# Unscaled wavelet columns, thresholds scaled on the chip, and evictions on ScalarE in a chain of four convolutions

## The chip, the cores and the metric

The kernel runs on one core of one Trainium2 chip. The metric is the device time of one execution in microseconds (us); lower is better. The core has these engines: TensorE (PE, with its weight loads shown as PEld), VectorE (DVE), ScalarE (ACT), GpSimd (POOL) and SyncE (SP), which here issues every DMA of the program from one queue. Each engine works through its own instructions in order and waits for others by semaphores.

## The reference

The input x has 4 images of 64 channels of 256 x 256, in float32. Four layers follow one another. Layers 0, 2 and 3 are long convolutions along rows and columns, each with a filter that a small network computes from positions; layer 1 works on Haar wavelet coefficients:

```
# layers 0, 2, 3: hx, hy are one row filter and one column filter per channel
k = einsum('ijk,imk->ijmk', hx, hy)[0]            # separable 256x256 filter
out = irfft2(rfft2(x, 512) * rfft2(k, 512) / 512)[..., :256, :256] + x * bias

# layer 1
f1 = haar2d(x)
for i in range(2):
    f3 = f1 * v[i]                                 # v, tau: one number per coefficient
    f4 = einsum('bchw,oc->bohw', f3, conv_w[i])    # mixes the 64 channels
    acc += sign(f4) * relu(abs(f4) - tau[i])       # soft threshold
out = haar2d(acc, inverse=True) + x
```

## The kernel before

Each convolution is a product with Toeplitz matrices, along rows and then along columns, on PE. Work goes in rounds of two channels of two images: a tile is [128, 8, 256], one "big" tile of 1 MB. Two groups of two images make 64 rounds.

**Phase A** (`phase_a`, loop over 64 rounds, each of ten "pieces") does layer 0 and the forward wavelet transform. A round's pieces 0 to 3 are row products (`rows`, PSUM tiles a1ps, copied to ay by ACT, L460), 4 and 5 the wavelet transform across rows of an earlier round (`product`, one small product with forward_sb into a3ps), 6 to 9 the column products (`columns`, a2ps). The transform along a row (`forward_free`) runs on POOL. The residual x * bias is added as DVE evicts a2ps (L480). The result of `product` is evicted by DVE with a multiplication by wrow, the orthonormal scale of each wavelet column (L493), and stored to the DRAM tensor coef. SP also loads x, two rounds ahead, and the Toeplitz matrices (toep, from filt in DRAM), and stores coef.

**Phase B** (`phase_b(grp)`, once for each group, 64 steps of two units) does the mixing. A unit's three pieces are: multiply by v and subtract thresholds of the unit before (`multiply` L642, `less` L662, both DVE), and add the unit before that to its sum on POOL; then the PE products of the next unit (`mix`, L623), the sign on ACT (L648) and the final max-times-sign on DVE (`threshold`, L667); then the magnitude on ACT (L657). The tile named a, of the magnitudes, and f4, of the PE products, are in PSUM, one buffer each in the first group. `load_v` fetches v and tau of a step in one DMA from one input, in which they alternate and each is repeated for the 64 channels.

**Phase C** (`phase_c`) does the inverse transform and layers 2 and 3, in rounds of 18 pieces. `inverse_free` undoes the row transform (POOL, and DVE for the first two rounds); there each level's differences are multiplied by sqrt(half), on ACT beforehand (`scales`, L378) or within a DVE operation (L403). Half of the second group's mixing results go to DRAM without threshold (`raw`), and phase C applies the threshold itself (`shrink`) with v and tau laid out by rows (`scale_rows`).

`beside(main, side, lead, tail)` writes the order out by hand: it issues the main pieces one after the other and puts the side pieces evenly between them, from main piece `lead` to `tail` pieces before the end. The order is: the network for layer 0; phase A's first 348 pieces beside `rest` (the networks of layers 2 and 3, and the stores of filters, filt<-padded); the following 272 pieces of phase A beside phase B of group 0; a transition; phase C beside phase B of group 1; phase C alone. In each piece `flush()` first issues the evictions that the piece before put off with `later`. Since nothing is reordered, an engine's queue holds the instructions in this order.

Of the kernel before, what the change touches and what calls it, by code (L numbers as in the profile page):

```python
# [41 lines left out]
F32 = mybir.dt.float32  # L42
AF = mybir.ActivationFunctionType
ALU = mybir.AluOpType
# [3 lines left out]
P = 128  # L48
B, C, N = 4, 64, 256

ROW = 64
# [48 lines left out]
def conv_haar_kernel(  # L100
    ctx: ExitStack, tc: tile.TileContext, x, zT, w1, wbd, cols, wo, decay, wo_first, decay_first, bias, forward, inverse, wrow, pack, v, v_rows, out
):
# [13 lines left out]
    unshrunk = coefficients("unshrunk")  # L116
    filt = [dram.tile([ROUNDS, 2, REPEATS, ITEMS, PERIOD], F32, tag=f"filt{l}", name=f"filt{l}") for l in range(NL)]

# [168 lines left out]
    nc.sync.dma_start(inverse_sb, inverse)  # L287
    wrow_sb = const.tile([P, N], F32, tag="wrow", name="wrow_sb")
    nc.sync.dma_start(wrow_sb, wrow.partition_broadcast(P))
    bias_sb = const.tile([P, NL * C], F32, tag="bias", name="bias_sb")  # L290
    nc.sync.dma_start(bias_sb, bias.partition_broadcast(P))

    for p in network([0]):
        p()

    rest = []
# [3 lines left out]
    for copy in spread(1, 0, ROUNDS, REPEATS // 2) + spread(2, 0, ROUNDS, REPEATS // 2):  # L300
        rest += [lambda: None] * (2 * APART - 4) + [copy]

    TILES = [(r, c) for r in range(2) for c in range(2)]

    def half(r):
        return slice(r * ROW, (r + 1) * ROW)

# [65 lines left out]

    def scales(src):

        half = 2
        while half < N:
            nc.scalar.mul(diffs(src, half), diffs(src, half), math.sqrt(half))  # L378
            yield
            half *= 2  # L380

    def inverse_free(src, dst, name, engine, level):


        blocks = src.rearrange("p n (k q) -> p n k q", k=BLOCKS)

        cur, half = blocks[:, :, 0:1, 0], 1
        while half < N:
            o = dst
            if half < HALF:  # L390
                o = level(2 * half)
            d = diffs(src, half)
            if half < BLOCKS:
                s, pair = cur, o.rearrange("p n (t q) -> p n t q", q=2)
            else:
                s = cur.rearrange("p n (k t) -> p (n k) t", k=BLOCKS)
                pair = o.rearrange("p n (k t q) -> p (n k) t q", k=BLOCKS, q=2)
            for q, op in ((0, ALU.add), (1, ALU.subtract)):
                to = pair[:, :, :, q]
                if engine is nc.gpsimd:  # L400
                    engine.tensor_tensor(to, s, d, op)  # L401
                else:
                    engine.scalar_tensor_tensor(to, d, math.sqrt(half) * (1 - 2 * q), s, ALU.mult, ALU.add)  # L403
                yield
            cur = o
            half *= 2
# [3 lines left out]
    def later(op):  # L410

        waiting.append(op)
# [23 lines left out]
    def phase_a():  # L436
# [45 lines left out]
        def product(t, bp):  # L482
            s = st[t]
            if bp == 0:

                s["f"] = big("out", f"f_{t}", 2)
            two = banks(f"a3ps{bp}_{t}")
            fw = blocks(s["fw"])
            haar(two, lambda r, c: fw[half(r), c, 2 * bp : 2 * bp + 2], forward_sb)
            for b, ps in enumerate(two):  # L490
                f = s["f"][:, 4 * bp + 2 * b : 4 * bp + 2 * b + 2]
                w = wrow_sb.unsqueeze(1).to_broadcast([P, 2, N])
                later(lambda f=f, ps=ps, w=w: nc.vector.tensor_tensor(f, ps, w, ALU.mult))  # L493

# [45 lines left out]
    def phase_b(grp):  # L540
# [25 lines left out]
        def load_v(s):  # L566
            if s >= STEPS:
                return
            d = st[s]
            d["v"], d["tau"] = [], []  # L570

            def fetch(first, count, tag):
                n = 2 * count * W
                t = bp.tile([P, count, 2, W], F32, tag=tag, name=f"{tag}_{grp}_{first}_{s}", bufs=3)
                at = v.offset + s * P * (4 * W + PAD) + first * 2 * W
                rows = bass.AP(v.tensor, at, [[4 * W + PAD, P], [1, n]])
                nc.sync.dma_start(t.rearrange("p i k w -> p (i k w)"), rows)
                d["v"] += [t[:, i, 0] for i in range(count)]
                d["tau"] += [t[:, i, 1] for i in range(count)]
# [121 lines left out]
        def piece(u, j):  # L701

            s, i = divmod(u, 2)
            if j == 0:
                if u < units:
                    multiply(u)
                if 0 < u <= units:
                    less(u - 1)
# [8 lines left out]
                if i and raw(2 * s - 1):  # L717
                    store(s - 1)
            elif j == 1:
                if u + 1 < units:  # L720
                    mix(u + 1)
# [34 lines left out]
    def phase_c():  # L756
# [389 lines left out]
```

## Time and profile before

| | us |
|---|---|
| median of 3 runs | 2545.4 |
| lowest and highest | 2540.11, 2548.39 |
| the profiled execution, its own time | 2543.18 |
| its span in the profile | 2541.3 |

| engine | busy us | share of the span | instructions |
|---|---|---|---|
| PE | 2311.6 | 91% | 53298 |
| PEld | 1875.9 | 74% | 53298 |
| DVE | 1840.0 | 72% | 2070 |
| ACT | 1325.9 | 52% | 2190 |
| POOL | 2063.0 | 81% | 2428 |

The span runs from the first to the last profiled instruction. The DMA engines moved 679.08 MB, 267 GB/s on average over the span. TensorE's granted clock was 0.979 of full speed on average. The shares are means over stages that have different limits, so the stretches of the span have to be looked at one by one. A row of the groups reads: line, engine, operation, output <- inputs, shapes, number; after the bar the busy time in us, the mean of one in ns, and the idle time of the engine just before them with what ended it. Busy times of neighbouring instructions overlap a little, so the distance between their starts is shorter than their durations.

### The profile page before, as it was taken

Reading aid. Unit: us, or ns where it says so; the run is one execution under the profiler, and the core shown is the slowest. Engines: PE = TensorE matmul, PEld = TensorE weight load, DVE = VectorE, ACT = ScalarE, POOL = GpSimd, SP = SyncE. Lnnn points to the kernel's source line nnn. Section 1 sums busy time; section 2 is a strip of 40 time slices with the busy share of each in tenths; the row PEclk is TensorE's granted clock in tenths of the full one; section 3 lists DMA queues with packets and bytes.
Section 4 is the critical chain, followed back from the end, with each engine's and each line's share of the span. In section 5 each row is a group of like instructions: output and inputs, shape, how many; then the busy total and the mean of one; then the engine's idle time right before and its main releaser. Section 6 shows DMA issues by size and latency. Waiting matters only on the chain.

```text
span 2541.3 us, 118857 instructions
## 1 busy us (share of the span) xinstructions
PE 2311.6 (91%) x53298; PEld 1875.9 (74%) x53298; DVE 1840.0 (72%) x2070; ACT 1325.9 (52%) x2190; POOL 2063.0 (81%) x2428
## 2 busy tenths in 40 slices
PE   7999998788888888877999999999989999999999
PEld 5799996444454444555777777787889999998888
DVE  4655557799999999856777677776667777777763
ACT  1122223566666666244666666666655555556552
POOL 2889997989899999768777767676779999999990
PEclk9999999899999999888999999999999999999999
DMA  6678877799999999556888889889866666666653
GB/s 201 224 269 271 272 275 296 266 327 338 337 320 341 336 318 340 206 184 248 318 320 313 306 302 321 311 312 315 287 215 217 216 215 217 215 212 207 220 167 111
DMA packets 201798, 679.08 MB, mean 267 GB/s; under 512 B 29119, under 2 KB 30464, under 8 KB 188873
## 3 DMA queue, kind: packets, MB, share of 16 engines
q1 hardware_dynamic: 201288, 671.48, 76.3%
q8 instruction: 419, 6.86, 1.1%
q14 instruction: 91, 0.74, 0.1%
HBM read 427.63 MB, written 243.73 MB: 264 GB/s over the span
## 4 chain that ended last, share of the span: by engine, by line
PE 44%; DVE 4%; issue 2%; ACT 2%; DMA 2%; POOL 2%; SPq 1%; DVEq 0%; ACTq 0%; POOLq 0%
PE c2c L312 10%; PE c2r L312 10%; PE c1r L312 9%; PE c1c L312 8%; PE c0ps L324 4%; PE f L623 3%; DVE cy L896 1%; DVE m L667 1%; DMA g<-mixed 1%; DVE x L642 1%; DVE x L662 1%; ACT ch L877 1%; POOL i L401 1%; ACT x L657 0%; SPq L161 0%
## 5 line engine op out<-in xcount | busy, mean ns | idle before, releaser
L401 POOL TENSOR_TENSOR i<-i,g 128x16 f32<-128x16 f32 x744 | 429.9, 598 | 28.2 <-ACT g L378 1.1
L312 PEld LDWEIGHTS a2ps<-toep,ay 64*64 64x64 f32 x8192 | 315.3, 136 | 126.3 <-DVE f L493 70.0
L623 PE MATMUL f<-ft,mix 64*64 64x512 f32 x2048 | 301.7, 623 | 116.8 <-DVE x L642 99.2
L312 PE MATMUL a2ps<-toep,ay 64*64 64x128 f32 (+3 forms) x8192 | 352.8, 303 | 27.4 <-DVE f L493 27.4
L312 PEld LDWEIGHTS a1ps<-toep,x 64*64 64x64 f32 x8192 | 300.1, 134 | 66.3 <-issue 31.8
L312 PE MATMUL a1ps<-toep,x 64*64 64x64 f32 (+3 forms) x8192 | 338.1, 299 | 4.3 <-DMA toep<-filt 2.3
L312 PEld LDWEIGHTS c2c<-toep,ch 64*64 64x64 f32 x8192 | 296.8, 135 | 61.0 <-issue 28.4
L312 PEld LDWEIGHTS c1c<-toep,ch 64*64 64x64 f32 x8192 | 295.4, 133 | 52.0 <-issue 23.7
L685 POOL TENSOR_TENSOR gt<-m,ft 128x512 f32<-128x512 f32 x128 | 163.3, 1276 | 197.8 <-DVE m L667 193.5
L312 PE MATMUL c1r<-toep,z 64*64 64x64 f32 (+3 forms) x8192 | 315.0, 300 | 7.8 <-issue 3.8
L312 PEld LDWEIGHTS c1r<-toep,z 64*64 64x64 f32 x8192 | 291.2, 135 | 41.5 <-issue 19.0
L312 PE MATMUL c2c<-toep,ch 64*64 64x128 f32 (+3 forms) x8192 | 310.0, 299 | 8.6 <-ACT ch L877 6.9
L312 PE MATMUL c2r<-toep,cy 64*64 64x128 f32 (+3 forms) x8192 | 310.1, 298 | 7.9 <-issue 6.6
L312 PEld LDWEIGHTS c2r<-toep,cy 64*64 64x64 f32 x8192 | 288.9, 134 | 37.6 <-issue 20.4
L401 POOL TENSOR_TENSOR ci<-i,g 128x1024 f32<-128x1024 f32 x124 | 312.1, 2539 | 4.5
L648 ACT ACTIVATE m<-x 128x1024 f32<-128x1024 f32 x194 | 206.0, 1062 | 210.0 <-DVE x L642 103.1
L312 PE MATMUL c1c<-toep,ch 64*64 64x128 f32 (+3 forms) x8192 | 307.3, 297 | 4.1 <-ACT ch L877 2.5
L460 ACT COPY ay<-a1ps 128x512 f32<-128x512 f32 x256 | 137.3, 589 | 325.2 <-PE a1ps L312 324.6
L877 ACT COPY ch<-c2r 128x512 f32<-128x512 f32 x256 | 137.2, 589 | 285.2 <-PE c2r L312 284.4
L493 DVE TENSOR_TENSOR f<-a3ps,wrow_sb 128x512 f32<-128x512 f32 x256 | 161.3, 682 | 122.5 <-PE a3ps L324 118.6
L642 DVE TENSOR_TENSOR x<-f,v 128x1024 f32<-128x1024 f32 x192 | 233.4, 1216 | 18.1 <-PE f L623 15.3
L896 DVE SCALAR_TENSOR_TENSOR o<-cy,bias_sb,c2c 128x512 f32<-128x512 f32 x256 | 176.9, 742 | 91.8 <-PE c2c L312 87.1
(84 smaller groups left out, 3950.7 us busy)
## 6 DMA issues: line engine op xcount, KB each, us to landing
toep<-filt SPq DMA_DIRECT2D x768, 112.0 KB
ft<-coef SPq DMA_DIRECT2D x128, 512.0 KB
v<-in_v SPq DMA_DIRECT2D x64, 1024.0 KB
mixed<-gt SPq DMA_DIRECT2D x128, 512.0 KB
g<-mixed SPq DMA_DIRECT2D x256, 256.0 KB
x<-in_x SPq DMA_DIRECT2D x128, 256.0 KB
coef<-f SPq DMA_DIRECT2D x128, 256.0 KB
x<-in_x SPq DMA_DIRECT2D x32, 1024.0 KB
```

The source lines that it names most:

```text
L312: nc.tensor.matmul(ps[r][half(c), j % 2, k * ROW :], data[half(r), c, k, bass.ts(j, ROW)], t(r, c)[:, : N - k * ROW], start=k == 0, stop=k ...
L324: nc.tensor.matmul(ps[r][half(c)].rearrange("p h k -> p (h k)"), matrix[half(r)], pairs(r, c).rearrange("p h k -> p (h k)"), start=True, s ...
L401: engine.tensor_tensor(to, s, d, op)
L460: later(lambda y=y, ps=ps: nc.scalar.copy(y, ps))
L493: later(lambda f=f, ps=ps, w=w: nc.vector.tensor_tensor(f, ps, w, ALU.mult))
L623: nc.tensor.matmul(un[u]["f4"][half(q), b, :], mixers[0][half(r), bass.ts(i, C)], st[s]["f"][half(r), b], start=True, stop=True, tile_posi ...
L642: nc.vector.tensor_tensor(un[u]["x"], un[u]["f4"], both(u, "v"), ALU.mult)
L648: nc.scalar.activation(un[u]["m"], un[u]["x"], AF.Sign)
L662: nc.vector.tensor_tensor(un[u]["a"], un[u]["a"], both(u, "tau"), ALU.subtract)
L685: nc.gpsimd.tensor_tensor(g[:, 0], m[:, 0], st[s]["f"][:, 0], ALU.add)
L877: later(lambda y=y, ps=ps: nc.scalar.copy(y, ps))
L896: nc.vector.scalar_tensor_tensor(to, of, bias_sb[:, at : at + 1], ps, ALU.mult, ALU.add)
```

## The change

The wavelet columns are no longer brought to orthonormal scale. The forward matrix for the rows is divided by sqrt(256) instead, L493 becomes a plain copy on ACT, and wrow is not loaded. A coefficient now has another factor in each column, so the threshold of that column needs the same factor: tau is loaded in a small form ([128, 1024]), multiplied on DVE by per_level once (`scale_thresholds`), and stored with 64 DMAs, each to four channels (`put_thresholds`), into a new DRAM tensor thresholds. These 65 pieces are merged evenly into `rest`. `load_v` fetches v from the input and tau from thresholds, in two DMAs into the two halves of one tile. In the inverse transform the differences are multiplied by half instead of sqrt(half). In the first group only, `less` moves from the first piece of a unit to the head of the second.

```diff
-    wrow_sb = const.tile([P, N], F32, tag="wrow", name="wrow_sb")
-    nc.sync.dma_start(wrow_sb, wrow.partition_broadcast(P))
...
+    def merged(one, other):
+        both = [((k + 0.5) / len(of), p) for of in (one, other) for k, p in enumerate(of)]
+        return [p for _, p in sorted(both, key=lambda x: x[0])]
...
+    tau_sb = mp.tile([P, 2, W], F32, tag="tau", name="tau_sb")
+
+    def scale_thresholds():
+        per_level_sb = mp.tile([P, N], F32, tag="per_level", name="per_level_sb")
+        nc.sync.dma_start(per_level_sb, per_level.partition_broadcast(P))
+        nc.sync.dma_start(tau_sb.rearrange("p r w -> p (r w)"), tau)
+        rows = tau_sb.rearrange("p r (h k) -> p (r h) k", k=N)
+        nc.vector.tensor_tensor(rows, rows, per_level_sb.unsqueeze(1).to_broadcast([P, 4, N]), ALU.mult)
+
+    def put_thresholds(copies, r, i):
+        of = tau_sb[half(i), r].unsqueeze(1).to_broadcast([ROW, copies.stop - copies.start, W])
+        nc.sync.dma_start(thresholds[:, r, copies, i * W : (i + 1) * W], of)
+
+    puts = [(slice(n, n + 4), r, i) for n in range(0, C, 4) for r in range(2) for i in range(2)]
+    rest = merged(rest, [scale_thresholds] + [lambda at=at: put_thresholds(*at) for at in puts])
...
-            nc.scalar.mul(diffs(src, half), diffs(src, half), math.sqrt(half))
+            nc.scalar.mul(diffs(src, half), diffs(src, half), half**power)
...
-                    engine.scalar_tensor_tensor(to, d, math.sqrt(half) * (1 - 2 * q), s, ALU.mult, ALU.add)
+                    engine.scalar_tensor_tensor(to, d, float(half * (1 - 2 * q)), s, ALU.mult, ALU.add)
...
-                w = wrow_sb.unsqueeze(1).to_broadcast([P, 2, N])
-                later(lambda f=f, ps=ps, w=w: nc.vector.tensor_tensor(f, ps, w, ALU.mult))
+                later(lambda f=f, ps=ps: nc.scalar.copy(f, ps))
...
             def fetch(first, count, tag):
-                n = 2 * count * W
-                t = bp.tile([P, count, 2, W], F32, tag=tag, name=f"{tag}_{grp}_{first}_{s}", bufs=3)
-                at = v.offset + s * P * (4 * W + PAD) + first * 2 * W
-                rows = bass.AP(v.tensor, at, [[4 * W + PAD, P], [1, n]])
-                nc.sync.dma_start(t.rearrange("p i k w -> p (i k w)"), rows)
+                t = bp.tile([P, 2, count, W], F32, tag=tag, name=f"{tag}_{grp}_{first}_{s}", bufs=3)
+                at = slice(first * W, (first + count) * W)
+                nc.sync.dma_start(t[:, 0].rearrange("p i w -> p (i w)"), v[s, :, at])
+                nc.sync.dma_start(t[:, 1].rearrange("p i w -> p (i w)"), thresholds[s].rearrange("r c w -> (r c) w")[:, at])
...
             if j == 0:
                 if u < units:
                     multiply(u)
-                if 0 < u <= units:
+                if 0 < u <= units and grp == GROUPS - 1:
                     less(u - 1)
...
             elif j == 1:
+                if 0 < u <= units and grp < GROUPS - 1:
+                    less(u - 1)
                 if u + 1 < units:
                     mix(u + 1)
...
-                for op in scales(late["rows"][:, k].rearrange("p s (h k) -> p (s h) k", h=2)):
+                for op in scales(late["rows"][:, k].rearrange("p s (h k) -> p (s h) k", h=2), (1.0, 0.5)[k]):
...
-    signs = signs * w[order][:ROW, None]
+    signs = signs * w[order][:ROW, None] / math.sqrt(N)
...
-        "v": padded(np.repeat(v[:, :, None], C, axis=2).reshape(STEPS * P, 4 * W)),
+        "v": padded(np.repeat(by_row("v")[:, :, None], C, axis=2).reshape(STEPS, P, 2 * W)),
+        "tau": f(by_row("tau").transpose(2, 0, 1, 3).reshape(P, 2 * W)),
+        "per_level": f((1.0 / (w[order] * math.sqrt(N))).astype(np.float32)),
```

More of the change, by code (lines that the diff above doesn't have):

```diff
@@ L100, in conv_haar_kernel @@
 def conv_haar_kernel(
-    ctx: ExitStack, tc: tile.TileContext, x, zT, w1, wbd, cols, wo, decay, wo_first, decay_first, bias, forward, inverse, wrow, pack, v, v_rows, out
+    ctx: ExitStack, tc: tile.TileContext, x, zT, w1, wbd, cols, wo, decay, wo_first, decay_first, bias, forward, inverse, pack, v, tau, per_level, v_rows, out
 ):
@@ L116, in conv_haar_kernel @@
     unshrunk = coefficients("unshrunk")
+    thresholds = dram.tile([STEPS, 2, C, 2 * W + PAD], F32, tag="thresholds", name="thresholds")
     filt = [dram.tile([ROUNDS, 2, REPEATS, ITEMS, PERIOD], F32, tag=f"filt{l}", name=f"filt{l}") for l in range(NL)]
@@ L294, in conv_haar_kernel, with half @@
         p()
+    def half(r):
+        return slice(r * ROW, (r + 1) * ROW)
+    def merged(one, other):
+        both = [((k + 0.5) / len(of), p) for of in (one, other) for k, p in enumerate(of)]
+        return [p for _, p in sorted(both, key=lambda x: x[0])]
     rest = []
@@ L301, in conv_haar_kernel @@
         rest += [lambda: None] * (2 * APART - 4) + [copy]
+    tau_sb = mp.tile([P, 2, W], F32, tag="tau", name="tau_sb")
[10 more added lines that the diff above has]
+    rest = merged(rest, [scale_thresholds] + [lambda at=at: put_thresholds(*at) for at in puts])
     TILES = [(r, c) for r in range(2) for c in range(2)]
-    def half(r):
-        return slice(r * ROW, (r + 1) * ROW)
     def toeplitz(ps, data, t, j):
@@ L372, in diffs, with scales @@
         return src.rearrange("p n (k q) -> p (n k) q", k=BLOCKS)[:, :, m : 2 * m]
-    def scales(src):
+    def scales(src, power=1.0):
         half = 2
         while half < N:
-            nc.scalar.mul(diffs(src, half), diffs(src, half), math.sqrt(half))
+            nc.scalar.mul(diffs(src, half), diffs(src, half), half**power)
             yield
@@ L572, in fetch @@
             def fetch(first, count, tag):
-                n = 2 * count * W
-                t = bp.tile([P, count, 2, W], F32, tag=tag, name=f"{tag}_{grp}_{first}_{s}", bufs=3)
-                at = v.offset + s * P * (4 * W + PAD) + first * 2 * W
-                rows = bass.AP(v.tensor, at, [[4 * W + PAD, P], [1, n]])
-                nc.sync.dma_start(t.rearrange("p i k w -> p (i k w)"), rows)
-                d["v"] += [t[:, i, 0] for i in range(count)]
-                d["tau"] += [t[:, i, 1] for i in range(count)]
+                t = bp.tile([P, 2, count, W], F32, tag=tag, name=f"{tag}_{grp}_{first}_{s}", bufs=3)
+                at = slice(first * W, (first + count) * W)
+                nc.sync.dma_start(t[:, 0].rearrange("p i w -> p (i w)"), v[s, :, at])
+                nc.sync.dma_start(t[:, 1].rearrange("p i w -> p (i w)"), thresholds[s].rearrange("r c w -> (r c) w")[:, at])
+                d["v"] += [t[:, 0, i] for i in range(count)]
+                d["tau"] += [t[:, 1, i] for i in range(count)]
             fetch(0, 2 if grp < GROUPS - 1 else 1, "v")
@@ L1090 @@
     scaled = signs * w[order][:ROW, None] / math.sqrt(N)
-    signs = signs * w[order][:ROW, None]
+    signs = signs * w[order][:ROW, None] / math.sqrt(N)
     pack = a["L1_conv_conv_w"].transpose(2, 0, 1).reshape(C, P)
-    v = np.stack([by_row("v"), by_row("tau")], axis=3)
     filters = [[[r * CI, r * CI + 1, C + r * CI + h] for h in range(2)] for r in range(ROUNDS)]
@@ L1129 @@
         "inverse": f(np.concatenate([scaled] * 2).astype(np.float32)),
-        "wrow": f(w[order].astype(np.float32)),
         "pack": f(np.concatenate([pack, pack])),
-        "v": padded(np.repeat(v[:, :, None], C, axis=2).reshape(STEPS * P, 4 * W)),
+        "v": padded(np.repeat(by_row("v")[:, :, None], C, axis=2).reshape(STEPS, P, 2 * W)),
+        "tau": f(by_row("tau").transpose(2, 0, 1, 3).reshape(P, 2 * W)),
+        "per_level": f((1.0 / (w[order] * math.sqrt(N))).astype(np.float32)),
         "v_rows": f(np.stack([by_block("v"), by_block("tau")], axis=1)),
```

## The prediction

> **What bounds the kernel now.** I read the busy time by stretch first, because the shares of the whole span mix four stages. I set the borders by the kernel's loops: the first convolution alone (to about 405 us), the same beside the first mixing (to 1020), a transition, the later convolutions beside the second mixing (1200 to 1830), and these alone. Columns: stretch, its length, busy us (instructions) of PE, PEld, DVE, ACT, POOL, granted clock, mean busy share of the DMA engines, GB/s.
>
> ```profile
> 62.00:153.00 91.00, 91.00 (x2244) 73.79 (x2240) 55.78 (x85) 18.24 (x34) 79.76 (x131) 1.00 0.67 235
> 153.00:362.00 209.00, 209.00 (x5444) 198.64 (x5438) 105.95 (x160) 42.95 (x80) 188.88 (x321) 1.00 0.81 273
> ...
> 500.00:1020.00 520.00, 423.75 (x6892) 251.85 (x6884) 497.01 (x508) 337.40 (x419) 472.03 (x518) 0.99 0.95 330
> ...
> 1200.00:1830.00 630.00, 589.61 (x13902) 491.00 (x13905) 455.13 (x431) 404.42 (x702) 450.83 (x511) 1.00 0.89 312
> ```
>
> In the first stage PE is never idle and DVE is half idle; the DMA engines have a fifth to a third left. In 500 to 1020, DVE is 96% busy, but the DMA engines are 95% busy too and POOL 91%. In 1200 to 1830 PE leads again, and the last stage has PE busy throughout.
>
> Next the costliest groups, for the prices, and the waits of 500 to 1000, for who is late (us in total, times, longest).
>
> ```profile
> L493 DVE TENSOR_TENSOR f<-a3ps,wrow_sb 128x512 f32<-128x512 f32 x256 | 161.3, 682 | 122.5 <-PE a3ps L324 118.6
> L460 ACT COPY ay<-a1ps 128x512 f32<-128x512 f32 x256 | 137.3, 589 | 325.2 <-PE a1ps L312 324.6
> ```
> ```profile
> PEld a2ps L312 <- DVE f L493: 51.3, 73, 2.0
> ...
> ACT a L657 <- DVE m L667: 90.7, 75, 2.5
> ACT m L648 <- POOL gt L682: 53.3, 31, 2.2
> ```
>
> DVE is waited for by PE and ACT; no engine's list in that window names a DMA (only SP's own queue does). So DVE sets the pace, with two other resources within 5%.
>
> Then the DMA engines' own rate for the kinds of transfer that resemble the new one. All stretches below have the engines over 90% busy. The first four hold a store filt<-padded (480 KB, from partitions 0 to 63, each read several times); the fifth holds coef<-f stores (also 64 partitions, but every second of 128); the last is in the mixing stage.
>
> ```profile
> 167.00:169.50 2.50, 2.50 (x81) 2.50 (x75) 0.42 (x1) 1.07 (x2) 2.05 (x3) 1.00 0.93 255
> 188.00:190.50 2.50, 2.50 (x81) 2.50 (x76) 0.41 (x1) 1.07 (x2) 2.01 (x2) 1.00 0.93 235
> ...
> 227.00:229.50 2.50, 2.50 (x83) 2.50 (x78) 1.78 (x4) 0.00 (x0) 2.15 (x9) 1.00 0.95 280
> ...
> 268.00:270.50 2.50, 2.50 (x86) 2.50 (x81) 1.41 (x2) 0.00 (x0) 2.26 (x8) 1.00 0.99 239
> 258.00:260.00 2.00, 2.00 (x68) 2.00 (x63) 1.41 (x2) 0.00 (x0) 1.76 (x6) 1.00 0.98 372
> ...
> 727.00:731.00 4.00, 3.95 (x88) 2.74 (x83) 4.00 (x6) 2.09 (x2) 4.00 (x3) 1.00 1.02 414
> ```
>
> Equally busy engines move 252 GB/s (mean of the first four) with the padded stores, and 372 to 414 without.
>
> **The change, part by part.**
>
> *64 threshold stores in the first stage.* Each takes 512 KB (524,288 bytes) from 64 neighbouring partitions of tau_sb, each row read four times, to DRAM in runs of 2 KB. The side list is spread over the pieces 2 to 318 of the first loop, ten a round: 65 items over 31.6 rounds, 2.03 stores a round. Every round's loads of x and toep and stores of coef stand behind them in SP's queue and in the DMA engines. The nearest row is the padded store: 524,288 / 252 GB/s = 2.08 us of all engines, 4.2 us a round. The coef stores' issues give the rounds: 20 from 153 to 361, 10.4 us each, of which 0.81 x 10.4 = 8.4 us are DMA; 8 from 62 to 153, 11.4 us each, of which 7.6 us. So a late round needs 8.4 + 4.2 = 12.6 us against 10.4, +2.2 us for 21 rounds = +46; an early one 11.8 against 11.4, +0.4 for 11 rounds = +4. Sum **+50**. Low end: all of a late round's bytes (273 x 10.4 + 2.03 x 524 KB = 3.9 MB) at 414 GB/s take 9.4 us, hidden under PE: 0. High end: the engines are no fuller than the 0.95 of the mixing stage: 12.6/0.95 = 13.3 and 11.8/0.95 = 12.4, 21 x 2.9 + 11 x 1.0 = +72. I take the padded row because source, queue, direction and repeated reading are the same; coef<-f differs in its partitions.
>
> The Trainium skill, "SBUF — State Buffer", section "Door 1: The DMA port swizzle", speaks against this part: partitions 0 to 63 (or 64 to 127) reach only 8 of 16 ports, measured there as 196 GB/s at 1 MiB, and two such transfers on different halves hardly overlap. By that a store would take 2.7 us, the stage would grow by some 90 us and the whole be 2612 instead of 2572, an estimate from the page; no row here shows such a transfer alone. It would also say why coef<-f, on every second partition, runs at 372.
>
> *Evictions from DVE to ACT.* 256 of 682 ns become copies, priced by L460 at 589 ns. In the first and last stages PE sets the pace: nothing. Beside the mixing a round takes 23.5 us, from the coef stores' issues:
>
> ```profile
> L497 SPq DMA_DIRECT2D coef<-f x44: 592/598/1442, 516.2 to 1009.5; - x44
> ```
>
> (two a round, 21 intervals). DVE: a pair occupies 1.20 us (it starts at 701.12, the next operation at 702.32), so 2.4 us leave 0.956 x 23.5 = 22.5: 20.1. ACT: 0.649 x 23.5 + 4 x 0.59 = 17.6. POOL stays at 0.908 x 23.5 = 21.3. The DMA engines stay at 0.95 x 23.5 = 22.3, for the same bytes are loaded. So the next thing late is the DMA: at 0.985 busy a round takes 22.65, -0.85 us for 26 rounds (1020 - 409 over 23.5) = **-22**. Ends: with POOL as the wall 21.3, -57 (the DMA rows' own time would have to shrink); on the other side, ACT works in order and an f copy now queues behind a sign that waits for POOL (up to 2.2 us) or a magnitude that waits for DVE (up to 2.5). PE's a2ps and the mixing matmuls behind it wait for that copy, and DVE for those. If both pairs of each round expose 2.5 us: 20.1 + 5.0 = 25.1, +42.
>
> *L662 moved to the head of the next piece, first mixing only.* It now stands behind the evictions, next to L667. It gets more time for its magnitude, but is no longer parted from L667, which reads its result: 1.34 us between their starts (714.16 to 715.50) instead of 1.15, about 0.2 us for three units in five, 5 units a round: +0.6 of DVE time. 20.7 is still under 22.3, so it costs nothing; without the DMA's cover it would cost 26 x 0.6 = 16. The v tile is freed, and SP's next load issued, one eviction pair (1.3 us) later; two steps of buffers (20 us) hide that.
>
> *Loads of v and thresholds, two instead of one.* One issue more (0.54 us on SP) a step, behind which ft, coef, toep and mixed stand; SP mostly waits for compute there. In the second mixing the rows halve to 2 KB. Bounds 0 to 57 steps x 0.54 = 31; PE leads, so nearest to nothing: **+2**.
>
> *Transition.* Between 1053 and 1078 five pairs of L493 stand between the L403 steps that end in ci: 6 us of DVE less at most, 0 at least where L403 waits for DMA or PE anyway: **-3**.
>
> *The start.* The wrow load goes, two small loads and one DVE product of 128x1024 (1.2 us as L642) come, while DVE idles half of the time: 0, ends -2 and +3. Factors in scales, inverse_free and scale_rows change value, not count: 0.
>
> Sum: 50 - 22 + 2 - 3 = +27. The profiled execution took 2543.2 us (span 2541.3 and 1.9 around it), 2.2 under the median of 2545.4: 2543.2 + 27 = 2570 beside its own time, **2572** beside the median.
>
> **The rivals.**
>
> 1. *The DMA engines swallow the stores* (not slower). Place: rounds 0 to 31. Price: the store's time p. For: 19% idle late, 33% early, and coef<-f at 372. Against: the 252 GB/s rows. The first stage grows by 21 x (2.03p - 2.0) us; it equals the 23 us won elsewhere at p = 1.53 us (343 GB/s), from where the change isn't slower. At p of 1.0 or less all is hidden: 2545 - 23 = 2522.
> 2. *A store at coef's price*: 524,288/372 = 1.41 us, 8.4 + 2.9 = 11.3, +0.9 x 21 = +19, less 23: 2541, no change.
> 3. *ACT takes DVE's place in the mixing*: PE's wait for f moves from DVE to ACT and grows; half of the +42 above and no gain: 2545 + 50 + 21 - 1 = 2615. For: four f copies stand in a row on ACT. Against: ACT is only 65% busy.
> 4. *The relief doesn't show* (the DMA wall at 0.95): 2545 + 50 + 2 - 3 = 2594.
>
> **How the numbers follow.** Main case (1.5 to 2.2 us a store, some relief) 0.52, its own range 2553 to 2590; rival 1 0.19; rival 2 0.13; rival 3 0.06; rival 4 0.10. About 0.3% (7.6 us) can be told from no change. Faster (below 2538): rival 1 and the lower edge of rival 2, 0.20. Same: most of rival 2, 0.13. Slower: the rest, 0.67. The range leaves out about 0.1 below and 0.1 above: 2528 to 2610.
>
> **What would show it.** In 153 to 400 the DMA share at 0.95 or more and PE no longer full, waiting for x or toep; the first L595 later than its 406 us by about 50 (the step is wrong if by under 20). Between that and the first L403 (643 us now) some 25 us less, DVE near 0.89 busy, DMA at 0.97 or more; a DMA share below 0.95 there with a shorter round would refute the wall. PE waiting for ACT f by more than the 51 us would speak for rival 3. The prediction fails altogether if the stores run above 343 GB/s.

## The result, and the profile after

The changed kernel takes 2637.74 us (median of 4 runs, 2635.87 to 2638.49); the kernel before took 2543.12 us beside it (median of 4, 2540.11 to 2548.39). The ratio is 1.037, 95% interval 1.035 to 1.039: slower by 3.7%. The profiled execution's span is 2635.8 us against 2541.3.

Four instants cut the span into stages: the start of the fifth round of phase A (its first ay copy); the first operation on tile spare_f, where the first mixing joins (L595 before, L616 after); the first operation of the inverse transform on i_x (L403 before, L426 after); and the end.

| us | fifth round | first stage ends | mixing, to the first i_x | i_x to the end | span |
|---|---|---|---|---|---|
| before | 68.2 | 406.3 | 643.1 | 1491.9 | 2541.3 |
| after | 81.0 | 517.8 | 645.8 | 1472.2 | 2635.8 |
| difference | +12.8 | +111.5 | +2.7 | -19.7 | +94.5 |
| forecast | | +50 | -22 | -1 | +27 |

The busy time by stretch of the kernel after, with the same columns as before (stretch, length, busy us and instructions of PE, PEld, DVE, ACT, POOL, granted clock, share of the DMA engines, GB/s):

```profile
62.00:153.00 91.00, 83.49 (x1872) 65.65 (x1875) 33.49 (x49) 30.00 (x58) 69.08 (x112) 0.96 0.89 277
153.00:500.00 347.00, 291.94 (x6670) 266.36 (x6666) 69.96 (x100) 99.32 (x194) 231.11 (x395) 0.94 0.88 275
500.00:1020.00 520.00, 393.98 (x6810) 269.76 (x6806) 420.32 (x405) 352.39 (x476) 455.87 (x510) 0.92 0.89 316
1200.00:1830.00 630.00, 576.82 (x13326) 466.07 (x13322) 444.51 (x427) 392.96 (x683) 471.34 (x521) 0.97 0.86 304
```

In the first stage PE, full before, stands still for 55 of 347 us and has a lower clock, yet the DMA engines are not full either: 0.88. (500 to 1020 now begins 18 us before the join, so it compares only roughly with the same stretch before.) The waits of PE in 153 to 500, and of all engines in a piece of the mixing, 640 to 840 (engine and line, whom it waited for: us in total, times, longest):

```profile
PE a1ps L335 <- DMA x<-in_x: 42.9, 29, 3.5
```
```profile
ACT a L678 <- DVE m L688: 42.6, 20, 3.1
...
PEld a2ps L335 <- ACT f L515: 29.4, 16, 4.5
...
DVE x L663 <- PE f L644: 23.0, 8, 4.0
PE a2ps L335 <- ACT f L515: 20.5, 8, 3.6
```

In the first stage PE waits for x to arrive. In this piece of the mixing PE waits for the eviction on ACT, eight times in eight rounds, and DVE, freed of the evictions, then waits for PE. The eviction itself got no dearer (L515's mean is 607 ns, L493's was 682); who waits for it shows in the costliest groups:

```profile
L335 PEld LDWEIGHTS a2ps<-toep,ay 64*64 64x64 f32 x8192 | 343.4, 140 | 126.6 <-ACT f L515 84.4
L335 PE MATMUL a2ps<-toep,ay 64*64 64x128 f32 (+3 forms) x8192 | 360.9, 312 | 51.5 <-ACT f L515 50.8
```

Before, the same two groups had waited 70.0 and 27.4 us for DVE's f.

The piece 640 to 840 does not stand for the whole mixing. By the starts of the ay copies, a round took 23.6 us before; after the change it takes 24.7 us from 621 to 868 us and 22.6 us from 868 to 1117. The stretch 900 to 1000, and PE's wait for the eviction in 930 to 1100:

```profile
900.00:1000.00 100.00, 77.35 (x1384) 51.25 (x1380) 90.14 (x85) 74.14 (x100) 93.71 (x100) 0.97 0.97 351
```
```profile
PE a2ps L335 <- ACT f L515: 7.4, 8, 1.3
```

So a loss in the first part of the mixing and a gain in the second nearly cancel in its +2.7 us.

### The profile page after: what moved, and what is told of

Its sections match the earlier page's. It is cut to its first block, busy times and chain, and to the rows that moved or that the text cites. A ratio compares the mean times of both kernels' runs of the same rounds, so it can differ in the third digit from the quotient of the medians.

```text
span 2635.8 us, 119315 instructions
## 1 busy us (share of the span) xinstructions
PE 2323.6 (88%) x53298; PEld 1950.2 (74%) x53298; DVE 1692.5 (64%) x1815; ACT 1450.0 (55%) x2446; POOL 2075.0 (79%) x2428
## 4 chain that ended last, share of the span: by engine, by line
PE 41%; DVE 4%; DMA 3%; ACT 2%; issue 2%; POOL 1%; SPq 1%; DVEq 0%; ACTq 0%; POOLq 0%
PE c2c L335 9%; PE c2r L335 9%; PE c1r L335 8%; PE c1c L335 8%; PE c0ps L347 4%; PE f L644 3%; DVE cy L919 1%; DVE m L688 1%; DMA toep<-filt 1%; DMA g<-mixed 1%; DVE x L683 1%; DVE x L663 1%; ACT g L401 0%; POOL i L424 0%; ACT x L678 0%
## 5 line engine op out<-in xcount | busy, mean ns | idle before, releaser
L335 PEld LDWEIGHTS a2ps<-toep,ay 64*64 64x64 f32 x8192 | 343.4, 140 | 126.6 <-ACT f L515 84.4
L644 PE MATMUL f<-ft,mix 64*64 64x512 f32 x2048 | 313.3, 632 | 123.4 <-DVE x L663 104.7
L335 PE MATMUL a1ps<-toep,x 64*64 64x256 f32 (+3 forms) x8192 | 353.9, 313 | 67.1 <-DMA x<-in_x 48.0
L335 PEld LDWEIGHTS a1ps<-toep,x 64*64 64x64 f32 x8192 | 316.5, 141 | 129.2 <-issue 70.1
L503 DVE SCALAR_TENSOR_TENSOR x<-x,bias_sb,a2ps 128x512 f32<-128x512 f32 x256 | 179.4, 742 | 337.8 <-issue 148.1
L335 PEld LDWEIGHTS c2c<-toep,ch 64*64 64x64 f32 x8192 | 306.5, 134 | 48.0 <-issue 24.7
L335 PEld LDWEIGHTS c1c<-toep,ch 64*64 64x64 f32 x8192 | 308.1, 134 | 42.4 <-issue 19.0
L335 PEld LDWEIGHTS c1r<-toep,z 64*64 64x64 f32 x8192 | 300.0, 135 | 28.9 <-issue 13.4
L335 PE MATMUL c2r<-toep,cy 64*64 64x192 f32 (+3 forms) x8192 | 313.8, 298 | 3.2 <-issue 3.2
L383 POOL TENSOR_TENSOR fw<-x 128x1024 f32<-128x1024 f32 x64 | 121.7, 1902 | 189.9 <-DVE x L503 187.6
```

The source lines that it names most:

```text
L335: nc.tensor.matmul(ps[r][half(c), j % 2, k * ROW :], data[half(r), c, k, bass.ts(j, ROW)], t(r, c)[:, : N - k * ROW], start=k == 0, stop=k ...
L383: nc.gpsimd.tensor_tensor(diffs, even, odd, ALU.subtract)
L503: nc.vector.scalar_tensor_tensor(to, old, bias_sb[:, c : c + 1], ps, ALU.mult, ALU.add)
L644: nc.tensor.matmul(un[u]["f4"][half(q), b, :], mixers[0][half(r), bass.ts(i, C)], st[s]["f"][half(r), b], start=True, stop=True, tile_posi ...
```

## The experiments

Each time in the table is from one execution beside one of the kernel before (2544.13, 2548.59 or 2558.12 us in the three sets). The stages come from the traces and agree within some 5 us between runs where nothing was changed in them: the first stage of the five kernels without stores ends at 406.9 to 411.6, and the mixing of the seven kernels with all copies on ACT, `less` moved and no row read eight times takes 645.8 to 649.8. In the kernels without stores the thresholds are not scaled, so their output is not the reference's. The whole, first:

| us | first stage ends | mixing | i_x to the end | time |
|---|---|---|---|---|
| no stores | 408.2 | 648.0 | 1472.1 | 2530.12 |
| stores from every second partition | 455.3 | 646.2 | 1472.9 | 2576.2 |
| stores from all partitions | 448.6 | 646.8 | 1474.4 | 2571.59 |
| eight rows stored | 429.1 | 686.6 | 1488.1 | 2605.55 |
| no stores, L683 back at the first piece | 407.4 | 673.8 | 1470.5 | 2553.51 |
| no stores, copies on DVE | 411.6 | 636.1 | 1481.1 | 2530.63 |
| small loads first | 507.0 | 648.0 | 1471.3 | 2628.1 |
| no stores, second pair on DVE | 406.9 | 648.8 | 1485.2 | 2542.77 |
| no stores, first pair on DVE | 409.4 | 610.2 | 1480.1 | 2501.57 |
| 32 stores, rows read twice | 424.2 | 649.8 | 1473.9 | 2549.71 |
| 64 stores, x in one load | 479.5 | 646.8 | 1468.5 | 2596.69 |

### The stores left out

The thresholds come from an input, in the layout in which the DRAM tensor had them; `scale_thresholds`, `put_thresholds` and their places in `rest` are gone.

```diff
-    rest = merged(rest, [scale_thresholds] + [lambda at=at: put_thresholds(*at) for at in puts])
...
+        "thresholds": padded(np.repeat(by_row("tau")[:, :, None], C, axis=2).reshape(STEPS, 2, C, 2 * W)),
```

> The changed kernel without the 64 threshold stores and the scaling: the thresholds come unscaled from an input, already repeated, so the output is not the reference's. Theory A (the stores lengthen the first stage): the first join of the mixing (L595 in the kernel before) moves back from 518 us to 406 +- 4, and the whole takes 2637.7 - 111 = 2527 +- 8. Rival (the evictions on ACT or the split loads also lengthen the first stage): the join stays above 420 and the whole above 2545. For the mixing stage: if its slow first half (24.7 us a round instead of 23.5) is left over from the late first stage, all of its rounds take about 22.7 here; if it belongs to the copies on ACT, half of them stay at 24.7.

Measured: the first stage is back at 408.2, the whole at 2530.12 us beside 2544.13. So the stores and the scaling cost 517.8 - 408.2 = 109.6 us, the whole excess of the first stage, and nothing elsewhere. The rest of the change gains nothing in the mixing (648.0 against 643.1, a loss of 5) and some 20 us after it.

### Where the stores read from

Two forms that write the same bytes. The first reads every second partition instead of 64 neighbours; the second reads all 128 partitions, with runs of 4 KB.

```diff
-        of = tau_sb[half(i), r].unsqueeze(1).to_broadcast([ROW, copies.stop - copies.start, W])
+        of = tau_sb.rearrange("(s i) r w -> i s r w", i=2)[i][:, r].unsqueeze(1).to_broadcast([ROW, copies.stop - copies.start, W])
```

> The same 64 stores of 512 KB in runs of 2 KB, but tau lies so that a store reads every second partition of 128 instead of 64 neighbours. Theory A1 (64 neighbouring partitions are the price, as with filt<-padded at 252 GB/s, and every second ones run at the 372 GB/s of coef<-f): a store costs 1.4 us instead of more than 2, the join comes at 425 to 450 instead of 518 and the whole takes 2545 to 2570. Rival A2 (33.5 MB more behind x and toep cost the same wherever they are read from): the join stays at 505 or later and the whole at 2625 or more.

```diff
+        of = tau_sb.rearrange("p r w -> p (r w)")
+        nc.sync.dma_start(thresholds.rearrange("s r c w -> (s r) c w")[:, n, : 2 * W], of)
...
+    puts = [(n,) for n in range(C)]
```

> 64 stores of 512 KB again, but each from all 128 partitions to one channel in runs of 4 KB. A1 (partitions): the join at 420 to 445, the whole at 2540 to 2565, and not much better than with every second partition. A third theory, A3 (short runs of 2 KB are the price): this one is clearly better than every second partition, by 20 us or more. A2 (bytes): the join at 505 or later.

Measured: every second partition brings the first stage to 455.3, 62.5 us less than 64 neighbours; all partitions with double the run length to 448.6, only 6.7 less again. The stretch 153 to 362 of the kernel after, with every second partition, and with all:

```profile
153.00:362.00 209.00, 175.37 (x3978) 159.22 (x3974) 41.84 (x60) 58.59 (x114) 144.15 (x248) 0.93 0.88 275
```
```profile
153.00:362.00 209.00, 193.58 (x4736) 173.97 (x4728) 49.87 (x72) 70.55 (x138) 164.80 (x285) 0.98 0.92 320
```
```profile
153.00:362.00 209.00, 195.65 (x4822) 176.11 (x4817) 49.21 (x70) 74.14 (x144) 168.88 (x284) 1.00 0.93 329
```

The last two numbers of each line carry it. At 0.88 busy the engines move 275 GB/s; at 0.92 and 0.93 they move 320 and 329. Per unit of busy share that is 313, 348 and 354 GB/s: the source partitions make most of the difference; the third form, which reads more partitions in longer runs, adds little. Per store, with the wait below included, the cost falls from 109.6/64 = 1.7 us to 47.1/64 = 0.74 (every second) and 0.63 (all).

### The wait at the start

Of the 111.5 us, 12.8 are there by the fifth round. DVE and SP in the kernel after, near 40 us (start, length, engine and line, operation, in brackets the idle time before and who ended it):

```profile
38.61 1.14 SPq L316 DMA_DIRECT2D per_level_sb<-in_per_level  x1
39.79 0.43 SPq L317 DMA_DIRECT2D tau_sb<-in_tau  x1
```
```profile
46.55 1.23 DVE L319 TENSOR_TENSOR tau_sb<-tau_sb,per_level_sb 128x1024 f32<-128x1024 f32 x1 [22.57 <-DMA tau_sb<-in_tau]
```

The small loads are issued only at 38.6 and 39.8, behind the loads of toep and x in SP's queue, and DVE, in order, stands at the scaling for 22.6 us, with the networks' work and the first residuals behind it. To test this, the two loads were put ahead of the filters:

```diff
     nc.sync.dma_start(bias_sb, bias.partition_broadcast(P))
+    per_level_sb = mp.tile([P, N], F32, tag="per_level", name="per_level_sb")
+    nc.sync.dma_start(per_level_sb, per_level.partition_broadcast(P))
+    tau_sb = mp.tile([P, 2, W], F32, tag="tau", name="tau_sb")
+    nc.sync.dma_start(tau_sb.rearrange("p r w -> p (r w)"), tau)
```

> The changed kernel with all its stores, but tau and per_level are loaded with the constants at the start instead of in the first round. In the changed kernel DVE stood at the scaling for 22.6 us, from 24 to 46.5, until tau had landed, and PE's fourth round began at 81 us instead of 68. Theory T (that wait costs some of the 111 us): the fourth round begins at 70 to 74, the join comes 7 to 13 us earlier (505 to 511) and the whole takes 2625 to 2631. Rival (the DMA makes up for it, since the stage is as long as its transfers): the join within 4 us of 518.

Measured: the first stage ends 10.8 us earlier (507.0), the whole is 9.6 us shorter (2628.1 against the median of 2637.74). So an edit costed at nothing cost about 10. The fifth round begins at 76.6, later than the 70 to 74 expected (which counts it as the fourth): only 4.4 of the 12.8 us have gone by then, and the rest of the gain comes later in the stage.

### The order in SP's queue

With the stores as in the changed kernel, x is loaded by one DMA of 1 MB a round instead of four of 256 KB.

```diff
-        n = CI if grp == 0 else 2 * M
+        n = 2 * M
```

> The changed kernel with all its stores and x loaded in one DMA of 1 MB a round in the first stage too, instead of four of 256 KB: the same bytes, three DMAs a round less. The stores cost about the 2.1 us of the engines that were reckoned, but the engines were only 0.89 busy while PE waited for x. Theory Q (what keeps them from being full is SP's queue, in order and with a limited number of transfers under way): fewer transfers fill them better, the share rises above 0.92 and the join comes 10 to 30 us earlier (488 to 508). Rival (the engines are as full as they get): the join within 5 us of 518.

Measured: the first stage ends 38.3 us earlier, at 479.5, with the same bytes from the same partitions. The stretch 153 to 362, to be read against 0.88 and 275 above:

```profile
153.00:362.00 209.00, 181.43 (x4379) 158.76 (x4375) 45.00 (x64) 65.92 (x128) 151.22 (x257) 0.98 0.93 302
```

What PE waits for in this stretch changes with it, first the kernel after and then one load:

```profile
PE a1ps L335 <- DMA x<-in_x: 28.6, 19, 3.5
```
```profile
PE a2ps L335 <- issue: 17.2, 10, 3.5
...
PE a1ps L335 <- DMA x<-in_x: 0.8, 2, 0.6
```

So transfers can be what PE waits for while the engines are 0.88 busy on average, and how x is divided in the queue changes that. With one load the wait for x is nearly gone; PE's idle time that is left is put down to "issue", where the profile names nothing that it waited for. Why the engines are only 0.88 busy is not shown. One reading is a circle: SP waits in order for ay and f on ACT, the transfers of x behind that start late, and PE's delay then delays ACT and SP. SP's own waits do not support it: they are 29 of 209 us in the kernel after, 49 with one load, where the rounds are shorter, and 54 in the kernel before, where PE is full. The last experiments below limit it further.

### Fewer rows stored, read more often

In the changed kernel every row of thresholds is stored once for each of 64 channels. Here eight are stored, and a load of the mixing reads each of them eight times; in the second form, which also has the small loads first and all partitions, 32 are stored and each is read twice.

```diff
-    puts = [(slice(n, n + 4), r, i) for n in range(0, C, 4) for r in range(2) for i in range(2)]
+    puts = [(slice(n, n + 4), r, i) for n in range(0, 8, 4) for r in range(2) for i in range(2)]
...
+                src = bass.AP(thresholds.tensor, thresholds.offset + s * 16 * row + first * W, [[row, 16], [0, 8], [1, count * W]])
```

> The thresholds are stored for 8 channels instead of 64 (8 stores of 512 KB instead of 64) and each load reads every stored row 8 times. All of A: the join at 406 + 111/8 = 420 at most, since an eighth of the stores is left. If reading a row again is as good as reading another, the mixing stages are as without the stores and the whole takes about 2530 to 2540; if repeated rows are slow, the mixing stage's DMA share is near 1, a round takes 24 us or more, and the whole is above 2560.

```diff
-    puts = [(slice(n, n + 4), r, i) for n in range(0, C, 4) for r in range(2) for i in range(2)]
+    puts = [(n,) for n in range(C // 2)]
...
+                src = bass.AP(thresholds.tensor, thresholds.offset + s * C * row + first * W, [[row, C], [0, 2], [1, count * W]])
```

> The changed kernel with tau loaded at the start, 32 stores of 512 KB instead of 64, each from all 128 partitions, and each load of thresholds reads every stored row twice. Half the bytes and no port limit: 64 such stores brought the join to 449 with the late tau, so 32 with the early one bring it to 412 to 425. Rows read 8 times lengthened the mixing stage by 40 us; if that comes from the repetition as such, twice costs 10 us or more (stage above 656), if it comes from many reads of one place, twice costs little (644 to 652). The whole: 2534 to 2556.

Measured: eight rows relieve the first stage (429.1, of which the wait at the start is a part) and cost 40.8 us in the mixing (686.6 against 645.8) and 15.9 after it (1488.1 against 1472.2). Reading twice costs nothing that can be told (649.8 against 648.0), with the first stage at 424.2. The mixing, 500 to 1020, with eightfold reading and with twofold:

```profile
500.00:1020.00 520.00, 389.61 (x6377) 256.52 (x6370) 420.56 (x390) 353.66 (x474) 439.99 (x485) 0.91 0.99 311
```
```profile
500.00:1020.00 520.00, 398.94 (x6818) 268.00 (x6816) 445.77 (x416) 374.89 (x501) 467.01 (x514) 0.94 0.95 331
```

Eightfold reading fills the engines (0.99) and moves less (311 GB/s): the same bytes have become dearer, and the engines are as good as full.

### L683 and the copies, each alone

From the kernel without stores: first L683 (`less`) back at the head of the first piece, then instead the copies on DVE.

```diff
-                if 0 < u <= units and grp == GROUPS - 1:
+                if 0 < u <= units:
                     less(u - 1)
```

> As without the stores (thresholds unscaled from an input, so the output is not the reference's), and the threshold subtraction stands in its old place, right after the multiplication. Without the stores the mixing stage of the first group takes 648 us from the first join to the first L403 (643 in the kernel before): its first ten rounds or so take 24.75 us, the later ones 22.7. Theory S1 (four copies f in a row on ACT, behind the magnitude and the exchange, hold PE up by 3.6 us a round while the hand-written order brings them together): no change of those first rounds, 24.75 +- 0.4. Rival S2 (the moved subtraction does it): all rounds at 22.7 to 23.2, the stage at 615 to 630.

```diff
-                later(lambda f=f, ps=ps: nc.scalar.copy(f, ps))
+                later(lambda f=f, ps=ps: nc.vector.tensor_copy(f, ps))
```

> As without the stores (output not the reference's), and the copies f are back on DVE, the subtraction where the change put it. S1: PE's wait of 3.6 us for f is gone, no two halves of the stage; DVE is the bound as before the change, a round takes 23.5 to 24.2 us and the stage 635 to 655. S2: the first rounds stay at 24.75 or longer, above 660 in all.

Measured, in the mixing: 643.1 before; 636.1 with `less` moved and copies on DVE; 648.0 with both parts of the change; 673.8 with copies on ACT and `less` where it was. Two of these comparisons differ in one edit alone: with copies on ACT, moving `less` gains 26 us (673.8 to 648.0); with `less` moved, bringing the copies to ACT loses 12 (636.1 to 648.0). The other two start from the kernel before and hold the split loads of v and thresholds too: 7 us gained by moving `less` with the copies on DVE (643.1 to 636.1), 31 lost by bringing the copies to ACT without it (643.1 to 673.8). The two parts are not independent, and the part that was to relieve DVE is the loss.

### Which copies

A round has two pairs of evictions. The piece order puts both pairs' products before the column products. In the kernel without stores, a round from 634 us on, ACT (L496 is the eviction there) and then PE:

```profile
636.18 1.08 ACT L464 COPY ay<-a1ps 128x512 f32<-128x512 f32 x2
638.07 1.06 ACT L650 ACTIVATE m<-x 128x1024 f32<-128x1024 f32 x1 [0.81 <-POOL gt L684]
639.03 1.01 ACT L659 ACTIVATE a<-x 128x1024 f32<-128x1024 f32 x1
640.07 1.25 ACT L675 COPY other<-ft 64x512 f32<-64x512 f32 x2
641.34 2.05 ACT L496 COPY f<-a3ps 128x512 f32<-128x512 f32 x4
```
```profile
634.14 1.37 PE L328 MATMUL a3ps<-fw,forward_sb 64*64 64x512 f32 x8
635.81 1.09 PE L625 MATMUL f<-ft,mix 64*64 64x512 f32 x8 [0.29 <-DVE x L644]
636.83 1.56 PE L328 MATMUL a3ps<-fw,forward_sb 64*64 64x512 f32 x8
641.98 2.46 PE L316 MATMUL a2ps<-toep,ay 64*64 64x256 f32 x26 [3.59 <-ACT f L496]
```

The first pair's product ends at 635.5. Its copies start only at 641.34: in ACT's queue they stand behind a sign that waits for POOL, a magnitude and the exchange copies. The column products want the PSUM banks of that pair, and PE stands 3.59 us. Two theories could explain this: four copies in a row are too many (then moving either pair helps), or the first pair alone, behind the sign, is late (then only moving the first helps).

```diff
-                later(lambda f=f, ps=ps: nc.scalar.copy(f, ps))
+                copy = nc.vector.tensor_copy if bp else nc.scalar.copy
+                later(lambda f=f, ps=ps, copy=copy: copy(f, ps))
```

> As without the stores (output not the reference's), with the first pair of copies f of a round on ACT and the second on DVE. S1: two copies in a row hold PE up less; the first rounds fall from 24.75 to 23.5 or less, the stage from 648 to 615 to 635 us. S2: the first rounds stay at 24.75.

```diff
-                later(lambda f=f, ps=ps: nc.scalar.copy(f, ps))
+                copy = nc.scalar.copy if bp else nc.vector.tensor_copy
+                later(lambda f=f, ps=ps, copy=copy: copy(f, ps))
```

> As without the stores (output not the reference's), with the first pair of copies f of a round on DVE and the second on ACT, the other way round from the run before. With the second pair on DVE PE waited for f just as long (17.5 us in 200, longest 3.6), so four copies in a row are not the cause. Theory S3 (the first pair is: PE's next column products reuse its PSUM banks, and on ACT it stands behind a sign, a magnitude and an exchange that wait in turn): PE's wait for f falls under 2 us each, no slow half, rounds of 22 to 23.5 us, the mixing stage of the first group 600 to 630 us instead of 648, the whole 2485 to 2515. Rival S4 (any load more on ACT slows its signs and magnitudes): rounds as with all copies on ACT, 24.7 and 22.7.

Measured: the second pair on DVE leaves the mixing as it was (648.8); the first pair on DVE brings it to 610.2. PE's waits for f in 640 to 840, with the second pair and with the first pair on DVE:

```profile
PE a2ps L316 <- ACT f L497: 17.5, 9, 3.6
```
```profile
PE a2ps L316 <- DVE f L497: 4.5, 4, 1.1
```

The theory of four in a row falls. The second part of the mixing fits the other: there, in the kernel without stores, a first pair starts at 922.37, right behind the sign and ahead of the magnitude and the exchange copies, and PE waits 1.26 us for it instead of 3.59. In that part all copies on ACT cost nothing: 22.8 us a round from 801 us on, against 23.4 with all of them on DVE. That points to the place in ACT's queue that the hand-written order gives the first pair. The piece 640 to 840 of the kernels before, after, and with the first pair on DVE:

```profile
640.00:840.00 200.00, 163.31 (x2638) 96.40 (x2634) 191.43 (x196) 130.30 (x163) 181.18 (x199) 0.98 0.95 333
```
```profile
640.00:840.00 200.00, 151.89 (x2536) 104.56 (x2538) 165.68 (x154) 139.26 (x188) 172.99 (x191) 0.91 0.91 316
```
```profile
640.00:840.00 200.00, 155.95 (x2814) 92.90 (x2808) 192.40 (x189) 146.00 (x189) 192.69 (x213) 1.00 0.97 352
```

After the change PE, DVE, POOL and the DMA engines are all less busy than before: the engines wait for one another. With the first pair on DVE, DVE and POOL are both 0.96 busy and the DMA 0.97: three resources end together, at 22.25 us a round.

### The findings together

One kernel with 32 stores from all partitions, rows read twice, the small loads first, x in one load, and the first pair on DVE; then two that keep the first stage's copies on ACT (the split only in the rounds beside the first mixing), with x in four loads and in one.

```diff
+                mixing = ROUNDS <= t < total - 4
+                copy = nc.vector.tensor_copy if mixing and bp == 0 else nc.scalar.copy
```

> Everything that helped, together, with the full computation: 32 stores from all 128 partitions, each row stored once and read twice by the mixing; the small loads ahead of the filters; x in one load; in each round the first pair of evictions on VectorE and only the second on ScalarE. If the three findings are independent (a queue short of engines, 64-partition stores, first pair behind the sign on ScalarE), the parts add up: the first L595 comes at 412 to 422 (32 stores alone: 424), the mixing takes 610 to 614 as with the first pair on VectorE alone (610.2), the rest 1474 to 1480; span about 2503, time about 2505, 0.985 of the kernel before. Rival: reading rows twice, which cost nothing while rounds were 24 us, shows now that the DMA engines are 0.97 busy: the mixing takes 620 to 635 and the whole 2515 to 2530. Second rival: the copies by VectorE come in the way of the first stage's residuals, and the first L595 comes after 430.

> As the run with everything together, but x again in four loads, and the first pair of evictions on VectorE only in the rounds beside the first mixing. If the single load is what delays the first stage when there are few stores: the first L595 at 424 (as with 32 stores and four loads: 424.2), the mixing 610, the rest 1472, span 2506, time 2508. If VectorE's evictions in the first stage did it: also 424 here, and the sister run with one load tells. If neither, but something in the tighter mixing: 432.

> The same with x in one load. If the single load delays the first stage (the store of the coefficients stands behind a load of 1 MB that it waits for): the first L595 at 430 to 434, DMA engines 0.83 busy, time 8 us above the sister run. If VectorE's evictions did it: 412 to 424, time at or under the sister run's.

| | first stage ends, us | mixing, us | median of 4 runs, us | ratio to before, 95% interval |
|---|---|---|---|---|
| all together, one load | 432.7 | 610.1 | 2518.02 | 0.989, 0.987 to 0.991 |
| split in the mixing, four loads | 419.0 | 609.4 | 2509.71 | 0.987, 0.984 to 0.989 |
| split in the mixing, one load | 432.6 | 609.2 | 2517.38 | 0.989, 0.986 to 0.992 |

The mixing's part adds up in all three, so twofold reading stays free even with the engines 0.97 busy. The first stage's does not: with 32 stores it ends at 432.6 and 432.7 in the two traces with one load, and at 419.0 and 424.2 in the two with four (the second is the run with 32 stores above). So with few stores the single load costs 8 to 14 us; the medians of the last two rows are 7.7 us apart, with ranges that overlap (2506.93 to 2513.21 and 2510.16 to 2521.81). VectorE's evictions in the first stage cost nothing (432.7 and 432.6). The stretch 153 to 362 with four loads and with one:

```profile
153.00:362.00 209.00, 204.58 (x5219) 183.92 (x5215) 53.43 (x76) 79.53 (x155) 181.49 (x307) 1.00 0.90 313
```
```profile
153.00:362.00 209.00, 196.41 (x4923) 172.34 (x4919) 50.63 (x72) 74.30 (x145) 171.18 (x289) 0.98 0.84 294
```

The engines' fullness again follows the grouping of x, but with the opposite sign (0.90 to 0.84, where 64 stores had 0.88 to 0.93). What is settled is that the division of x in the one queue moves the first stage by 8 to 38 us at the same bytes; why one load helps in the one case and hurts in the other is open. In the one-load kernel the trace names no DMA among the things PE waited for. SP waited longer there: in 68 to 410, 55.3 us for f on ACT and 45.2 us for DVE to be done with an x buffer, against 14.0 and 13.5 with four loads; whether that is the cause or a consequence is not shown. The version with four loads is the shortest of them, 1.3% under the kernel before.

## Why the prediction was wrong

The direction was right; the size was not, and 2637.7 lies above the range. By the steps of the sum:

- **Stores, +50 forecast, +111.5 measured: the step that failed.** The price of a store in engine time agrees with the forecast: a late round took 14.2 us (mean of 22 rounds from 160 us on) at 0.88 busy, 12.5 us of the engines, where 12.6 were forecast. (It is no constant: with one load of x the same bytes took 12.9 us at 0.93, 12.0 us of the engines.) What failed is the step from engine time to elapsed time: the sum divided by 1, and its high end by "no fuller than the 0.95 of the mixing stage". At 0.88, 12.6/0.88 = 14.3 us, and 21 x 3.9 = 82 us; with the 12.8 us up to the fifth round that is most of the 111.5. The six rounds from 81 to 160 us, 13.1 each where 11.8 were forecast and 11.4 were taken before, add 10. A share taken from a stage with another order of transfers was used as a limit here. That the stores are the cause is shown by leaving them out; why the engines got no fuller than 0.88 is open beyond what the source partitions (62.5 us) and the division of x (38.3 us) account for, each changed alone; the last experiments show that such gains need not add up.
- **The start, 0 forecast.** "DVE idles half of the time" was true of the average and beside the point: an in-order engine stands at an instruction whose load is late, and the load was issued at 39.8 us. Measured +10.
- **The source partitions.** Every second partition instead of 64 neighbours takes 62.5 us off, at 348 instead of 313 GB/s per unit of busy share. The Trainium skill, "SBUF — State Buffer", section "Door 1: The DMA port swizzle", by which partitions 0 to 63, or 64 to 127, reach half of the ports, spoke against this part, and these runs agree with it. The estimate by the page, 2612, was nearer than mine. The prediction had both rows, 252 and 372 GB/s, and took the price from one without asking what made them differ.
- **Evictions to ACT, -22 forecast, +12 measured by themselves.** The prediction wrote down the mechanism that decided ("an f copy now queues behind a sign that waits for POOL ... PE's a2ps and the mixing matmuls behind it wait for that copy") and gave it a chance of 0.06 as rival 3, because ACT is only 65% busy. The busy share was no evidence: the wait comes from the place in the queue. Its "four f copies stand in a row" was the wrong detail; the first pair alone does it. In the second part of the mixing, where the first pair has a better place, a round takes 22.6 us with the DMA engines 0.97 busy, where 22.65 at 0.985 were forecast; in the first part it takes 24.7. So the round came out as forecast where that wait is short, and the wait of the first part, which the sum left out, used up the gain.
- **The DMA wall at 22.3 us a round.** Not a fixed wall: with the first pair on DVE the same bytes (352 GB/s x 22.25 us = 7.8 MB, before 333 x 23.5 = 7.8 MB) took 0.97 x 22.25 = 21.6 us of the engines. Busy share times round length was not a fixed cost of the bytes.
- **`less`, 0 forecast, -26 measured with the copies on ACT** (-7 with them on DVE, a comparison that holds the split loads too). The prediction saw that its magnitude gets more time and counted that as nothing. In 640 to 840, with the copies on ACT, DVE's wait for the magnitude is 18.8 us with `less` in its old place and 9.4 with it moved, which fits; but PE's wait for f falls with it (26.8 to 17.6), so how much of the gain comes from there is not shown.
- **After the mixing, -1 forecast (split loads +2, transition -3), -19.7 measured.** The stretch from the first i_x operation to the second group's first spare_f shrank from 62.2 to 50.1 us, and 7.6 us came later. Copies on DVE give back 9 (1481.1 against 1472.1; 8 and 13 with one pair of them there), so about half of it goes with DVE freed of the evictions. The other half was not taken apart.

Of the signs named in advance, the DMA share of 0.95 or more in 153 to 400 failed (0.88), PE waiting for x came true (42.9 us), the mixing shorter by 25 us at a DMA share of 0.97 failed (2.7 longer, 0.89 in 500 to 1020), and the wait for ACT f above 51 us came true in the window in which it was named, 500 to 1000, where PE's weight loads waited 68.1 us for it.

## What to carry to other kernels

Engine time of added transfers is only the floor of their cost: divide by the fullness that the queue reaches in that stage with that order, and look at which partitions they read. Before an operation is moved to a less busy engine, find what stands ahead of it in that engine's queue and who waits for its result; here the second of two pairs of evictions could move and the first could not. A small operation put early in an in-order engine holds up what stands behind it until its latest input has come, however idle the engine is on average: here DVE stood for 22.6 us, and the kernel lost about 10.

## What the runs showed of the hardware

- Stores of the same bytes ran at 275 GB/s and a busy share of 0.88 from 64 neighbouring partitions, and at 320 GB/s and 0.92 from every second of 128 (153 to 362).
- Reading a row of DRAM eight times in one load made the engines 0.99 busy at 311 GB/s (500 to 1020); reading it twice cost nothing (348 GB/s at 0.97 in 640 to 840 of the best version).
- TensorE's granted clock did not follow its busy share: in 640 to 840, with the copies on DVE, it was busy for 148.6 us, its longest matmul wait was 1.7 us, and it was granted 0.99; without stores it was busy for 154.6 us with waits of up to 3.6 us once a round, and was granted 0.94. The longest wait alone does not settle it either: with x in one load, in 153 to 362, PE had waits of up to 3.5 us and was granted 0.98.
- The DMA engines moved 352 GB/s over 200 us of the mixing at a share of 0.97; 333 at 0.95 had looked like their end.
